# Attention and a feed-forward network on one core: the stream turned by VectorE and through DRAM ahead of the normalisation

## The chip, the cores and the metric

The kernel runs on one core of a Trainium2 chip. The metric is device time in microseconds (us), the median of several runs. A profiled execution gives a trace of every instruction on the core's engines: TensorE (PE, matrix products; PEld is its loading of weights), VectorE (DVE), ScalarE (ACT), GpSimd (POOL), and SyncE (SP), whose queue issues all the DMAs of this kernel.

## The reference, cut to what matters

The input x has 8 batches of 512 tokens and 256 features. It is normalised, and two branches work on it: a causal attention with one head (`s`), and a small transformer of two layers (`g`). The output is `x + s * silu(g)`. The 8 x 512 x 256 input runs through each layer of the transformer as follows, batch by batch:

```python
h = shift_token(x)                    # second half of the features comes from the token before
q, k, v = split(h @ wqkv)             # 8 heads of 64; q and k normalised, scaled, rotated
x = x + local_attention(q, k, v) @ wo # windows of 128 tokens, looking one window back
h = shift_token(x)
h = (h - mean) / sqrt(var + 1e-5) * lg + lb
a, g = split(h @ w1 + b1)             # 682 features each
x = x + (a * gelu(g)) @ w2 + b2
```

All arithmetic is in fp32. The change touches the step between the second `shift_token` and the product with `w1`.

## The kernel before, in words

**Layout.** The stream of one batch, `xT`, lies in SBUF with features on the 128 partitions: two chunks of 128 features, each with 512 tokens as columns. The second chunk begins one column earlier than its data, on a column of zeros, so that reading columns `c * T` to `(c + 1) * T` gives the shifted token stream at no cost. Mean and variance run over features, though, which lie on partitions; so the feed-forward must turn the stream to tokens on partitions, normalise it, and turn it back before the product with `w1`.

**The turns in the feed-forward (lines 1021 to 1191).** For each pair of token tiles (2 x 128 tokens), TensorE makes four 128x128 transposes of `xT` into a PSUM bank, `hps` (lines 1087 to 1094; the transpose itself is line 304). `layernorm` (line 438) then reads that bank: `bn_stats` and `bn_aggr` on VectorE, two small steps on GpSimd for the reciprocal root, and one `tensor_scalar` per tile on VectorE that writes `xh` in SBUF (tag `tok`, two buffers). Back it goes without TensorE, in `blocks_back` (line 1050): VectorE turns each pair in 32x32 blocks into `hn`, four DMAs write `hn` to DRAM (`hn_away`, 128 KB each), one DMA of 512 KB reads it back into `hn` with the blocks in place, and ScalarE applies gain and bias. Then come six steps of `ff` products with gelu, and two of `w2p` products, which add to the stream. The last feed-forward (batch 7, layer 1) runs in two halves and turns back on TensorE; the other fifteen work on a whole part.

**The same pattern elsewhere.** The local attention turns its q, k and probabilities this way too: VectorE in blocks, away to DRAM (`away`, `p_away`), and back in place (`qT`, `kT`, `pT`). All of these DMAs stand in SP's one queue.

**What sets the order.** The work is split into jobs written as generators; each `yield` names what its next step needs (events, free buffers, a time). The string `ORDER` (line 42) gives the order of all TensorE work: each letter is a job, and each occurrence runs it to its next `yield`; a number repeats it. A is the products with `wo` (`wop`), B the weighted sums (`ops`), C the reading back of probabilities, D the scores (`sps`), E the reading back of q and k, F the projections (`qkv`), G late loads of weights. From H on, letters are the start of a batch (normalisation and the one-head attention), the feed-forwards and the finishing steps: I is the feed-forward of batch 0, layer 0, and j that of batch 6, layer 1. I write (6,1) for batch 6, layer 1. B and D use TensorE as an array of 64x64 parts ("quarters"), the other steps use the full array.

The instructions of the other engines and the DMAs are placed by a planner, `Order.on` (line 141), at the time at which its model has their data ready; the planned order on each engine is then fixed by dependencies (`keep`, line 153). The planner's times are written in the code: `TURN_512` for a block turn of 512 columns, `LAND` for the landing of DMAs by KB (line 640), 0.42 us for an issue on SP in `send` (line 336). Each engine works through its queue in that order, so an instruction that waits holds up those behind it.

**Buffers.** There are 8 PSUM banks, one `hn`, one `hid`, two `tok`, four `xT`.

Of the kernel before, what the change touches and what calls it, by code (L numbers as in the profile page):

```python
# [15 lines left out]
P = 128  # L16
BATCH = 8
T = 512
# [21 lines left out]


ORDER = (
    "H2JH5FHFHF2JEHEF2NH3EHGHFHF3H2FH2ED2HEJ2EGF2JCFGCD2NCEF2E2J2BDCDFJEC2FEJ2EBFJDEGCJCFJFCD"
    "F2EARJEAJBGCFCJ2FEFCIJFEJ2BDGDFJGCAECEFINENCN2AI2NRNFBDIN2F2N2DN2IC3IEI5EDEBDNEI2DNF3NE"
    "F2ECDNC2ANF2ABKENCFCNCFR4DRDBERFKR2EKFEAEC2RCAKDRF2RFRKDE2F4EDEDBCFCKCECK3EBDCEDRFECFAFR"
    "FKACDEBCLCDKCFEF2BFCKCE2F3EALRD2LAKEFLCEKDBRC2FEF2LRDBELF4D2CA2ECELCL2EFLBEDODEC3F3ECLBF"
    "LA2CD2O2CF2O2CFE3FL2BCECDRFRF2EFOBDCM3EC2OMOFDEDMF2VEA2CO2EFOBC2DF2EF2BDVPOF2EV2CEAPAVFE"
    "PD2CEPOEPVFCFVOBD2FCVFEVEVEFCVECP3EBCD2VCF2A2ECFPFPEDCBDEC2F3CEFBP2FES2A2VD2E2FSPVCFC2S"
    "F2DBC2PFEVEQFVSFBDE2V2EFCQ2CQFCASVD2ESATS2F2QBEDC3DVFSZBF3S2CVEFCTFECZF2E2A2D2BT2Z2FSEZE"
    "ZC2ZCSTD2E2BZCF2ZF2CTFADCDFTZFETE2ATBEDEDF2C4FTET2FD2EWBZFCTEFECFZA2WZW3ZCFTBD2ZFE2ZCFE"  # L50
    "C2WFUFUZUEW2EUDBDZWEF2CACFCFAEZDBDZUFCFE2XCFW3CFZBDCEdDFCFXAFAWd2E2XFCdEdFBXdC2dWXD2BEX"
    "F2EdCF2dDCEDFEdA2CdFEFCX2aBC2XFDBFDdF2CFXCX2aE2dE2Fd2CaAEFdAD2EBXFD2aEC2F2CaFdEXEBC2dF2E"
    "YEaYFCFY2A2FD2BCYChF3CabFa2EaEadDBDhCFAF2EdEFCaAdb2FbDEbhDhE2aChaBDbCE2FDFCbCEbCFDBDE2C3"
    "F2hEAbFAhbFBD2CeCEF2b2FeBeF2E3C3AhAF2ehF2DEFDEFCehb2D2BFE3e2C3e2EBCD2E2eCF2A2CfFc2FhBCDE"
    "DcCFCFeFBeEhFEF2Af2AC2cEDEDFfCEheFeBCfEDChF4BfEDhFCEf2D2EcECFCfEAFAfFDiBDC3EfFEfhBEF3iAC"
    "hACiFi2FD2ChEfF2E3fDCEBDiFiCiCECi4D2BC2i2AF3gAjCjEBC2F2EFhEBjFEA2FgFjFDFEhFjDCFED2F2jCE"
    "C2EjEj2BE2CgCjFDBDCjAEjAhlDgDl2C2j2lBlglC2k2Cl4BklAkAn3lknlnm2n2mn3o2n2ono"
)


# [180 lines left out]
def gated_attention_kernel(  # L241
# [78 lines left out]
    def event(*key):  # L320
        return events.setdefault(key, {})
# [11 lines left out]
        arrived[""] = max(arrived[""], order.clock() + 2.0) + dst.free_size() * dst.shape[0] * 4 / 0.34e6  # L333
        arrived[name] = arrived[""]

    def send(dst, src, after, us):

        sync.dma_start(dst, src)
        return order.on("SP", 0.42, after) + us

    x_tiles = {}

# [92 lines left out]
    def inv_sqrt(dst, src, n):  # L435
        gpsimd.tensor_tensor(dst, src, neg_half[:, 0:n], ALU.pow)

    def layernorm(dst, src, n, name, at=0.0, groups=False):


        kind = name[0]
        few = 2 if kind == "x" else 4
        stats = small.tile([P, n, 6], F32, tag=f"stats{kind}", name=f"stats_{name}", bufs=few)
        mv = small.tile([P, n, 2], F32, tag=f"mv{kind}", name=f"mv_{name}", bufs=few)
        for i in range(n):
            vector.bn_stats(stats[:, i], src[:, i])
            end = order.on("DVE", 0.41, at, opens=f"stats{kind}")
        for i in range(n):
            vector.bn_aggr(mv[:, i], stats[:, i])
            at = order.on("DVE", 0.16, end, opens=f"mv{kind}")  # L450
        rstd = small.tile([P, n], F32, tag=f"rstd{kind}", name=f"rstd_{name}", bufs=few)
        gpsimd.tensor_scalar(rstd[:, 0:n], mv[:, 0:n, 1], EPS, None, ALU.add)
        at = order.on("POOL", 0.23, at, opens=f"rstd{kind}")
        inv_sqrt(rstd[:, 0:n], rstd[:, 0:n], n)
        at = order.on("POOL", 0.4 + 0.16 * n, at)
        for i in range(n):
            to, some = dst[:, i], src[:, i]
            if groups:
                to = to.rearrange("p (g c b) -> p c g b", g=4, c=KC)
                some = some.rearrange("p (c g b) -> p c g b", g=4, c=KC)  # L460
            vector.tensor_scalar(
                to, some, mv[:, i, 0:1], rstd[:, i : i + 1], ALU.subtract, ALU.mult
            )
            end = order.on("DVE", 0.54 if kind == "h" else 0.41, at, opens="tok" if kind == "h" else "")
        return end


# [169 lines left out]
    qTs, kTs, vs = {}, {}, {}  # L637


    TURN_512, LAND = 0.79, {64: 2.6, 128: 2.4, 256: 2.9, 384: 4.0, 512: 4.6}  # L640

    def project(b, l, t):

# [377 lines left out]
    def feed_forward(b, l, part):  # L1021
# [17 lines left out]
        def need(tag):  # L1039
            return {} if part.start else {tag: 1}  # L1040

        def behind(tag):
            return [event(tag, b, l)] if part.start else []

        def gained(dst, src, c):
            scalar.activation(
                dst, src, AF.Identity, bias=bias[:, c : c + 1], scale=gain[:, c : c + 1]
            )

        def blocks_back(hn, ends):  # L1050
# [25 lines left out]

        pairs = range(part.start // (2 * P), part.stop // (2 * P))
        yield {"after": [event("windowed", b, l, part.start), event("loaded", l, 1)]}
        yield {"after": behind("hn"), "free": need("hn") | {"tok": len(pairs)}}
        xT = stream[b]  # L1080
        hn = common("hn", [P, KC, T])
        xh = {t2: buffer("tok", [P, 2, DIM], f"xh_{b}_{l}_{t2}") for t2 in pairs}
        ends = {}
        for t2 in pairs:
            windowed = [event("windowed", b, l, t2 * 2 * P)]
            yield {"after": windowed, "free": {"bank": 1}}
            hps = bank(f"hps_{b}_{l}_{t2}").rearrange("p (a f) -> p a f", a=2)
            for a in range(2):
                t = 2 * t2 + a
                for c in range(KC):  # L1090
                    transpose(
                        hps[:, a, c * P : (c + 1) * P],
                        xT[:, c * T + t * P : c * T + (t + 1) * P],
                    )
            at = layernorm(xh[t2], hps, 2, f"h_{b}_{l}_{t2}", groups=whole_part)
            ends[t2] = at
            free(f"hps_{b}_{l}_{t2}", at)
        if whole_part:

            hn, at = yield from blocks_back(hn, ends)  # L1100
# [267 lines left out]
```

## Time and profile before

| | |
|---|---|
| time, median of 3 runs | 1326.94 us (1324.37 to 1330.78) |
| profiled execution, its own time | 1327.62 us |
| its span, first to last instruction | 1325.7 us |
| granted TensorE clock | 0.994 |
| busy: PE, DVE, ACT, POOL | 1297.2, 1041.5, 750.2, 623.8 us |
| DMA packets, bytes | 396884, 209.49 MB |

Busy times are those of one execution. A group of instructions is given with its engine and operation, what it writes and reads, its shape and count, then its busy time and the mean length of one in ns, and the idle time of the engine just before it with what ended that. Matmuls overlap in TensorE's pipeline: what one costs is read from start to start. In lists of waits the columns are the total in us, the number of times, and the longest.

### The profile page before, as it was taken

The page shows a single profiled execution, that of the slowest core. Times are in us where ns is not written, and L with a number is a line of the kernel's source. Part 1 is how long each engine was busy: PE and PEld are TensorE (multiplying, and loading weights), DVE is VectorE, ACT ScalarE, POOL GpSimd, SP SyncE. Part 2 cuts the span into 40 slices and gives each one's busy share as a digit, 9 for nine tenths or more (in the row PEclk, how much of TensorE's full clock was granted, in tenths as well). Part 3 has the DMA queues.
Part 4 walks back from the last instruction along what each step waited for, and adds up shares of the span by engine and source line. Part 5 has one row for each costly group of instructions (what it writes and reads, how often), then busy time and mean ns, then how long its engine had stood idle before and what let it go on. Part 6 is the DMA issues. An engine that isn't in the chain of part 4 may idle for free.

```text
span 1325.7 us, 29785 instructions
## 1 busy us (share of the span) xinstructions
PE 1297.2 (98%) x10498; PEld 752.9 (57%) x10498; DVE 1041.5 (79%) x3092; ACT 750.2 (57%) x1954; POOL 623.8 (47%) x651
## 2 busy tenths in 40 slices
PE   9989999999999999999999999999999999999898
PEld 4556556555555565555555655555555555555466
DVE  6778677888688987887878787788888897866764
ACT  2553554765656465563657646555655657562764
POOL 6647336564454544545543545555345354416400
PEclk9989999999999999999999999999999999999999
DMA  5878535766667564676467665575755686545662
GB/s 188 238 191 223 139 83 132 185 172 156 160 160 186 127 173 117 182 189 165 114 144 196 163 145 140 127 204 139 177 135 141 165 204 159 139 126 129 171 156 80
DMA packets 396884, 209.49 MB, mean 158 GB/s; under 512 B 153880, under 2 KB 382400, under 8 KB 396736
## 3 DMA queue, kind: packets, MB, share of 16 engines
q1 hardware_dynamic: 396736, 207.59, 62.3%
q8 instruction: 84, 1.38, 0.4%
q14 instruction: 64, 0.52, 0.1%
HBM read 111.56 MB, written 95.94 MB: 157 GB/s over the span
## 4 chain that ended last, share of the span: by engine, by line
PE 83%; DMA 6%; DVE 4%; SPq 3%; ACT 2%; POOL 2%; issue 1%; DVEq 0%; ACTq 0%
PE qkv L300 20%; PE ff L300 20%; PE w2p L300 12%; PE wop L300 7%; PE sps L300 6%; PE ops L300 5%; PE qk L300 3%; SPq L70 3%; PE av L300 2%; DMA qT<-away 2%; PE sc L300 2%; PE v0p L300 2%; DMA x<-in_x_dram 1%; PE hps L304 1%; ACT p L70 1%
## 5 line engine op out<-in xcount | busy, mean ns | idle before, releaser
L70 POOL TENSOR_TENSOR r<-r,side 128x512 f32<-128x512 f32 x128 | 162.8, 1271 | 454.4 <-DVE side L70 437.1
L300 PE MATMUL qkv<-wqkv,xT 128*128 128x512 f32 x768 | 357.8, 599 | 0.1
L300 PE MATMUL ff<-hn,w 128*128 128x512 f32 (+1 forms) x680 | 283.5, 568 | 0.0
L70 ACT ACTIVATE p<-p,nmx 128x192 f32<-128x192 f32 (+1 forms) x512 | 219.4, 429 | 89.5 <-DVE nmx L70 88.9
L300 PEld LDWEIGHTS qkv<-wqkv,xT 128*128 128x128 f32 x768 | 141.2, 191 | 140.5 <-issue 128.8
L70 POOL TENSOR_TENSOR rn<-ss,neg_half 128x8 f32<-128x8 f32 x128 | 212.9, 1664 | 10.7
L300 PEld LDWEIGHTS ff<-hn,w 128*128 128x128 f32 x680 | 128.1, 190 | 137.2 <-issue 122.8
L300 PE MATMUL w2p<-hid,w 128*128 128x512 f32 (+3 forms) x408 | 159.8, 577 | 0.0
L70 DVE CUSTOM_DVE_ANT_0 p<-sps,mask_sb 128x192 f32<-128x192 f32 (+1 forms) x512 | 146.7, 331 | 13.6 <-PE sps L300 13.3
L70 ACT ACTIVATE p<-p,rden 128x192 f32<-128x192 f32 (+1 forms) x282 | 118.6, 434 | 44.3 <-DVE rden L70 42.3
L70 DVE STREAM_TRANSPOSE pr<-p 128x384 f32<-128x384 f32 (+1 forms) x256 | 128.9, 527 | 16.7 <-ACT p L70 11.6
L70 POOL TENSOR_TENSOR r<-r,rn 128x512 f32<-128x512 f32 x128 | 134.2, 1048 | 10.0
L70 ACT ACT_TABLE_LOAD x99 | 127.0, 1283 | 4.5 <-DMA out_dram<-g 2.1
L70 ACT ACTIVATE sq<-qkv 128x512 f32<-128x512 f32 x128 | 75.2, 592 | 93.9 <-PE qkv L300 87.3
L70 DVE SCALAR_TENSOR_TENSOR hid<-ff,vec,hid 128x512 f32<-128x512 f32 (+3 forms) x119 | 83.1, 710 | 52.4 <-PE ff L300 29.9
L300 PE MATMUL wop<-oT,wo 128*128 128x256 f32 x512 | 119.1, 380 | 0.0
L300 PE MATMUL sps<-kT,qT 64*64 64x128 f32 (+1 forms) x3584 | 106.1, 255 | 11.8 <-ACT p L70 4.8
L300 PEld LDWEIGHTS sps<-kT,qT 64*64 64x64 f32 x3584 | 90.4, 136 | 44.5 <-issue 23.1
L300 PEld LDWEIGHTS w2p<-hid,w 128*128 128x128 f32 (+1 forms) x408 | 68.6, 189 | 79.5 <-issue 77.5
L300 PEld LDWEIGHTS wop<-oT,wo 128*128 128x128 f32 x512 | 96.4, 190 | 29.2 <-issue 14.7
L70 DVE TENSOR_TENSOR r<-qkv,tables 128x512 f32<-128x512 f32 x128 | 86.4, 675 | 31.5 <-ACT sq L70 29.2
L70 ACT ACTIVATE hid<-ff,vec 128x512 f32<-128x512 f32 (+2 forms) x102 | 65.7, 661 | 69.3 <-PE ff L300 68.6
(83 smaller groups left out, 1710.6 us busy)
## 6 DMA issues: line engine op xcount, KB each, us to landing
pT<-p_away SPq DMA_DIRECT2D x96, 384.0 KB, 4.3
away<-rt SPq DMA_DIRECT2D x256, 128.0 KB, 2.6
p_away<-pr SPq DMA_DIRECT2D x256, 128.0 KB, 2.3
kT<-away SPq DMA_DIRECT2D x64, 256.0 KB, 3.1
qT<-away SPq DMA_DIRECT2D x256, 64.0 KB, 2.9
p_away<-pr SPq DMA_DIRECT2D x192, 64.0 KB, 2.0
pT<-p_away SPq DMA_DIRECT2D x32, 256.0 KB, 3.3
hn_away<-hn SPq DMA_DIRECT2D x60, 128.0 KB, 2.4
```

The lines of the kernel that those rows point to most:

```text
L70: ins = getattr(self.engine, name)(*args, **kwargs)
L300: nc.tensor.matmul(out, lhsT=lhsT, rhs=rhs, start=start, stop=stop)
L304: nc.tensor.transpose(out, in_, ident)
```

## The change

For a whole part, the turn to tokens on partitions leaves TensorE. A new inner function `blocks_out` waits until both halves of the attention's output have been added to the stream. VectorE turns the two chunks of the stream in 32x32 blocks into `hn`, four DMAs write those to a DRAM tile `h_away` laid out as 512 tokens by 256 features, and two DMAs of 256 KB read it back, one per pair of token tiles, into `xh`. `layernorm` then works in place on `xh` in SBUF, for one pair after the other. The rest, `blocks_back` included, is as before. `layernorm` loses its `groups` argument, `send` gains `opens`, three landing times of the planner are changed, and `ORDER` is a new sequence over the new steps (a feed-forward on a whole part now has 15 of them, 14 before). The last feed-forward keeps its turns on TensorE.

```diff
 ORDER = (
...
-    "DcCFCFeFBeEhFEF2Af2AC2cEDEDFfCEheFeBCfEDChF4BfEDhFCEf2D2EcECFCfEAFAfFDiBDC3EfFEfhBEF3iAC"
-    "hACiFi2FD2ChEfF2E3fDCEBDiFiCiCECi4D2BC2i2AF3gAjCjEBC2F2EFhEBjFEA2FgFjFDFEhFjDCFED2F2jCE"
-    "C2EjEj2BE2CgCjFDBDCjAEjAhlDgDl2C2j2lBlglC2k2Cl4BklAkAn3lknlnm2n2mn3o2n2ono"
...
+    "f2BfA2iciEihi2F2EC2FECFhEcFfhFDBDFEF2E3fcC2i3D2CECi3giBD2C2i2FAF2AEBC3FjFEFEhBFA2j2Ejgj"
+    "F4jDF2EhDECEjDFCDh2gFCEhFEj2CBgCDCDjEjECBEjCjA2DCDl3j2lCBClglCl3klkBlA2kn3lklnkm2n4mn2o2"
+    "n2ono"
 )
...
-    def send(dst, src, after, us):
+    def send(dst, src, after, us, opens=""):
 
         sync.dma_start(dst, src)
-        return order.on("SP", 0.42, after) + us
+        return order.on("SP", 0.42, after, opens=opens) + us
...
         for i in range(n):
-            to, some = dst[:, i], src[:, i]
-            if groups:
-                to = to.rearrange("p (g c b) -> p c g b", g=4, c=KC)
-                some = some.rearrange("p (c g b) -> p c g b", g=4, c=KC)
             vector.tensor_scalar(
-                to, some, mv[:, i, 0:1], rstd[:, i : i + 1], ALU.subtract, ALU.mult
+                dst[:, i], src[:, i], mv[:, i, 0:1], rstd[:, i : i + 1], ALU.subtract, ALU.mult
             )
...
-    TURN_512, LAND = 0.79, {64: 2.6, 128: 2.4, 256: 2.9, 384: 4.0, 512: 4.6}
+    TURN_512, LAND = 0.79, {64: 2.6, 128: 2.6, 256: 3.1, 384: 4.4, 512: 4.6}
...
+        def blocks_out(hn, ends):
+
+
+            yield {"after": [event("windowed", b, l, t2 * 2 * P) for t2 in pairs]}
+            mine = hn.rearrange("p c n -> p (c n)").rearrange("p (k c a) -> p k c a", c=KC, a=32)
+            for c in range(KC):
+                src = xT[:, c * T : (c + 1) * T].rearrange("p (k a) -> p k a", a=32)
+                vector.transpose(mine[:, :, c], src)
+                at = order.on("DVE", TURN_512, opens="" if c else "hn")
+            away = dram.tile([T, DIM], F32, tag="h_away", name=f"h_away_{nm}", bufs=4)
+            rows = away.rearrange("(k a) (g n) -> g a k n", a=32, g=4)
+            mine = mine.rearrange("p k c a -> p k (c a)")
+            for g in range(4):
+                left = send(rows[g], mine[g * 32 : (g + 1) * 32], at, LAND[128])
+            tiles = away.rearrange("(t p) f -> p t f", p=P)
+            for t2 in pairs:
+                yield {"at": left - 1.0, "free": {"tok": 1}}
+                xh[t2] = buffer("tok", [P, 2, DIM], f"xh_{b}_{l}_{t2}")
+                landed = send(xh[t2], tiles[:, 2 * t2 : 2 * t2 + 2], left, LAND[256], "tok")
+                ends[t2] = layernorm(xh[t2], xh[t2], 2, f"h_{b}_{l}_{t2}", landed)
+
...
         yield {"after": [event("windowed", b, l, part.start), event("loaded", l, 1)]}
-        yield {"after": behind("hn"), "free": need("hn") | {"tok": len(pairs)}}
+        yield {"after": behind("hn"), "free": need("hn") | ({} if whole_part else {"tok": 1})}
         xT = stream[b]
         hn = common("hn", [P, KC, T])
-        xh = {t2: buffer("tok", [P, 2, DIM], f"xh_{b}_{l}_{t2}") for t2 in pairs}
-        ends = {}
-        for t2 in pairs:
...
+        xh, ends = {}, {}
+        if whole_part:
+            yield from blocks_out(hn, ends)
+        else:
+            for t2 in pairs:
...
+                at = layernorm(xh[t2], hps, 2, f"h_{b}_{l}_{t2}")
```

More of the change, by code (lines that the diff above doesn't have):

```diff
@@ L42 @@
 ORDER = (
[L43 to L54, printed above, removed]
@@ L55 @@
-    "DcCFCFeFBeEhFEF2Af2AC2cEDEDFfCEheFeBCfEDChF4BfEDhFCEf2D2EcECFCfEAFAfFDiBDC3EfFEfhBEF3iAC"
-    "hACiFi2FD2ChEfF2E3fDCEBDiFiCiCECi4D2BC2i2AF3gAjCjEBC2F2EFhEBjFEA2FgFjFDFEhFjDCFED2F2jCE"
-    "C2EjEj2BE2CgCjFDBDCjAEjAhlDgDl2C2j2lBlglC2k2Cl4BklAkAn3lknlnm2n2mn3o2n2ono"
+    "H3JH2FH3GFH2F4H2JHNEF2EHFH3EGEF3HEDHFDEHCFHJ3CDECEDFCEJFENJ2ED2BCGEJCJFJCFJFBD2CJRFJ2FCF"
+    "EGCEA2EBIJIGFJEFJC2GF2JDFBDEJCFEJFA2GI2NEN2CINRNDCN4BNDNFEIN2IEF2NCECD2NEIECI5BD2I2AF2NF"
+    "NCEFNC3FAFKFEBNCERCKR4EDBDEF3EFC2RCA2KD2FRKCF3EFEK2FBRCECFEDERBDCKFERECFCA2F2ED2RFK2EREC"
@@ new lines @@
+    "KD2BFCF2CE2KFK2BDLDRCF2ACECELCEFALFKBCDCDKRL2BECEFEF2RLC2FAFEFAFLD2EBFEF2CLFLCODCDEL2E2F"
+    "L2EBCD2ROAC2F3AEOEOFCFBEORF2D2ROE2C2FRL2BD2CFOACEMAEFCEFM3FEO2BD2CFMEF2EFVC3O2EO2DBDF3EF"
+    "EOVPAC2PVAV2P2EFV2CBDC2DOCFP2BVE2CVF2CAFED2CE2F2AFPBFE2VCP2FCSFD2FVEP2BDCDVFVC2PF2ACAPSE"
+    "BSCESECVFE2PD2BFESF2PVF2EAQC2VCV2ADS2EDFQBQ2C2TFEF3VS2CQFZSD2EBS3FEFCFEAEAET2CVTCF2D2ZVZ"
+    "FZSTZ2TZE2SBCTEDC2FDFZEZCFBDF3DEZCFETCA2E2CT2DBCDECFETF3BD2TC2FWCETFAWAE2FZCBWZCFZCTDEDB"
+    "ZFCFWTWCZEFZFAECWFAFUFZUFBD2ZFE2F2WC2UXEWCWEWUD2WFE2WZWUCdBD2ZFECZCFCEFXEAWFdADXdDXBdC2F"
@@ new lines @@
+    "WXEBCdCFE2d3CAFAFD2BdXEFECF4CdXdaEXFCEFXFDBDEFEF2X2C2AED2CdAFE2X2CFaEadDaDBEFCdCaXFCXBdF"
+    "EYF2CdYEadYCFEA2D2aCYBECYFECFEaFaFDbDdEFa2BhF2aFEFACaAEdD2EbEC3baDabDBCdCFdF2bEhEbFEBbhC"
+    "FChCFhAFEADBFDFhCECFebFEbDEDCEhb2FBECDCDEFbFCFbEA2CFEe2Fhe2BFCDCF2beDCE2BEFCEF2bD2CFE2e"
+    "A2eCeEeDBC2DcFEF2feFBD2eCeCAfAEFEFChfFEFef2CEBDC2hFeEDEBFhFhCcfFfFAD2hAECECF3fEfCfBCiDCD"
+    "f2BfA2iciEihi2F2EC2FECFhEcFfhFDBDFEF2E3fcC2i3D2CECi3giBD2C2i2FAF2AEBC3FjFEFEhBFA2j2Ejgj"
+    "F4jDF2EhDECEjDFCDh2gFCEhFEj2CBgCDCDjEjECBEjCjA2DCDl3j2lCBClglCl3klkBlA2kn3lklnkm2n4mn2o2"
@@ L436, in inv_sqrt, with layernorm @@
         gpsimd.tensor_tensor(dst, src, neg_half[:, 0:n], ALU.pow)
-    def layernorm(dst, src, n, name, at=0.0, groups=False):
+    def layernorm(dst, src, n, name, at=0.0):
         kind = name[0]
@@ L456, in layernorm @@
         for i in range(n):
-            to, some = dst[:, i], src[:, i]
-            if groups:
-                to = to.rearrange("p (g c b) -> p c g b", g=4, c=KC)
-                some = some.rearrange("p (c g b) -> p c g b", g=4, c=KC)
             vector.tensor_scalar(
-                to, some, mv[:, i, 0:1], rstd[:, i : i + 1], ALU.subtract, ALU.mult
+                dst[:, i], src[:, i], mv[:, i, 0:1], rstd[:, i : i + 1], ALU.subtract, ALU.mult
             )
-            end = order.on("DVE", 0.54 if kind == "h" else 0.41, at, opens="tok" if kind == "h" else "")
+            end = order.on("DVE", 0.54 if kind == "h" and dst is not src else 0.41, at, opens="tok" if kind == "h" and dst is not src else "")
         return end
@@ L1078, in feed_forward @@
         yield {"after": [event("windowed", b, l, part.start), event("loaded", l, 1)]}
-        yield {"after": behind("hn"), "free": need("hn") | {"tok": len(pairs)}}
+        yield {"after": behind("hn"), "free": need("hn") | ({} if whole_part else {"tok": 1})}
         xT = stream[b]
         hn = common("hn", [P, KC, T])
-        xh = {t2: buffer("tok", [P, 2, DIM], f"xh_{b}_{l}_{t2}") for t2 in pairs}
-        ends = {}
-        for t2 in pairs:
[L1085 to L1097, printed above, removed]
+        xh, ends = {}, {}
[3 more added lines that the diff above has]
+            for t2 in pairs:
+                xh[t2] = buffer("tok", [P, 2, DIM], f"xh_{b}_{l}_{t2}")
+            for t2 in pairs:
+                windowed = [event("windowed", b, l, t2 * 2 * P)]
+                yield {"after": windowed, "free": {"bank": 1}}
+                hps = bank(f"hps_{b}_{l}_{t2}").rearrange("p (a f) -> p a f", a=2)
+                for a in range(2):
+                    t = 2 * t2 + a
+                    for c in range(KC):
+                        transpose(
+                            hps[:, a, c * P : (c + 1) * P],
+                            xT[:, c * T + t * P : c * T + (t + 1) * P],
+                        )
+                at = layernorm(xh[t2], hps, 2, f"h_{b}_{l}_{t2}")
+                ends[t2] = at
+                free(f"hps_{b}_{l}_{t2}", at)
         if whole_part:
```

## The prediction

> **What bounds the kernel now.** I began with the busy shares on the profile's page:
>
> ```profile
> PE 1297.2 (98%) x10498; PEld 752.9 (57%) x10498; DVE 1041.5 (79%) x3092; ACT 750.2 (57%) x1954; POOL 623.8 (47%) x651
> ...
> q1 hardware_dynamic: 396736, 207.59, 62.3%
> ```
>
> TensorE (PE) is busy for all but 28.5 us of the 1325.7 us span. The view of busy time by stretches says where those are (columns: length, PE busy, PE loads, DVE, ACT, POOL, clock, DMA share, GB/s):
>
> ```profile
> 0.00:120.00 120.00, 108.24 (x760) 64.49 (x761) 89.05 (x270) 53.25 (x154) 77.34 (x91) 0.96 0.75 214
> 400.00:800.00 400.00, 397.67 (x3316) 229.21 (x3315) 332.08 (x985) 234.91 (x609) 192.92 (x198) 1.00 0.64 158
> 1200.00:1325.70 125.70, 116.02 (x946) 77.05 (x944) 81.47 (x223) 68.04 (x148) 37.16 (x40) 0.98 0.52 135
> ```
>
> Of the idle time 11.8 us lie in the first 120 us and 9.7 us in the last 125.7; the 1080 us between have 7.0. In the middle TensorE is the bound, and work taken from it comes back as time unless something new makes it wait. The view of waits, for TensorE alone (total, times, longest), shows which waits could grow:
>
> ```profile
> PE sps L300 <- ACT p L70: 4.8, 2, 3.6
> PE sps L300 <- DMA qT<-away: 4.6, 5, 2.0
> PE ops L300 <- DMA pT<-p_away: 4.5, 6, 1.3
> ```
>
> The wait for `hps` data (the stream, written by VectorE) is only 0.8 us in all. The groups by shape price what is removed and added, the DMA list prices the transfers (KB each, median us from issue to landing):
>
> ```profile
> L70 DVE STREAM_TRANSPOSE rt<-r 128x512 f32<-128x512 f32 x128 | 90.2, 704 | 17.4 <-POOL r L70 10.2 <-DMA away<-rt 5.9
> L70 DVE TENSOR_SCALAR xh<-hps,mv_h,rstd_h 128x256 f32<-128x256 f32 x64 | 31.5, 533 | 4.6 <-POOL rstd_h L70 4.5
> L70 DVE TENSOR_SCALAR x<-x,mv_x,rstd_x 128x256 f32<-128x256 f32 x32 | 14.4, 508 | 0.8 <-POOL rstd_x L70 0.8
> L304 PE MATMUL hps<-ident,xT 128*128 128x128 f32 x128 | 20.1, 279 | 0.8 <-DVE xT L70 0.8
> kT<-away SPq DMA_DIRECT2D x64, 256.0 KB, 3.1
> qT<-away SPq DMA_DIRECT2D x256, 64.0 KB, 2.9
> hn_away<-hn SPq DMA_DIRECT2D x60, 128.0 KB, 2.4
> ```
>
> A mean of 279 ns overstates a turn on TensorE, since they are pipelined. The timeline of TensorE gives what four of them take from start to start:
>
> ```profile
> 924.77 0.60 PE L304 MATMUL hps<-ident,xT 128*128 128x128 f32 x4
> 925.20 1.88 PE L300 MATMUL qkv<-wqkv,xT 128*128 128x512 f32 x4
> 926.92 0.60 PE L304 MATMUL hps<-ident,xT 128*128 128x128 f32 x4
> 927.45 1.57 PE L300 MATMUL sps<-kT,qT 64*64 64x128 f32 x64
> ```
>
> Four turns hold TensorE for 0.437 us (the times unrounded); before a 64x64 step 0.530.
>
> **What the Trainium skill says.** "VectorE: DVE Perf Modes", section "The three transpose paths": TensorE turns a full 128x128 into PSUM, VectorE only 32x32 blocks, into SBUF. The trace agrees: `hps` is a PSUM bank, `rt` and `hn` are SBUF tiles, and their blocks are put in place by DMA. The same page, "The perf-mode tier table", gives fp32 `tensor_scalar` from SBUF twice the rate that a PSUM source allows. The trace does not show that: 508 ns from SBUF (`x`) against 533 ns from PSUM (`xh`); I use 508. "DMA: Bandwidth & Descriptors", section "Specifications": below 512 B a transfer is under line rate. The trace agrees in direction: 64 KB in 128-byte pieces (`qT`) land in 2.9 us, 128 KB in 1 KB rows (`hn_away`) in 2.4. "Perfetto Trace Analysis", "DMA Instruction — HWDGE (DVE, Sync)": a DMA's wait is made by the sequencer that issues it. The trace agrees: SP's own queue stood 61.4 us, in 53 waits, for `away<-rt` to land.
>
> **The change, part by part.** Fifteen of the sixteen feed-forwards work on a whole part; the last keeps the old path.
>
> *Removed from TensorE:* 15 x 8 = 120 turns, 30 bursts x 0.437 = **-13.1 us**. If the dearer bursts (0.49 to 0.53) are real savings, up to -14.8; that is the low end.
>
> *The new sequence.* I went through both strings letter by letter, with the kind of TensorE work of each step. Changes between full-array and split-array work rise from 187 to 195. A visit to the 64x64 steps costs 0.12 going in or out (the first turn after `sps` starts 149 ns after the last `sps` instead of 28), 0.055 more on that burst (0.492) and 0.09 the other way (0.530 less 0.437): 0.27 for both ways, 0.13 a change. 8 x 0.13 = **+1.1 us**.
>
> *VectorE:* two more 128x512 turns per feed-forward, 30 x 0.70 = 21 us; four normalising steps per feed-forward from SBUF, 60 x (533 - 508 ns) = -1.5 us. VectorE goes from 79% to about 81%; in the stretch 400 to 800, with 332 of 400 us busy, to some 85%. I cost it at nothing on the path: its cover is the 17% that stay idle there. If that cover is gone where the masks of `sps` queue behind the two turns, each feed-forward could lose up to 1.4 us, 21 us in all (high end); nothing excludes zero.
>
> *DMA and SP:* each feed-forward had five issues (four `hn_away`, one `hn`); it gets six more, four writes and two reads, 90 in all. The trace has 1346 issues with 669 us of SP time, 0.5 us each: +45 us, SP from 50% to 54%. Packets: 2048 of 256 B and 512 of 1 KB per feed-forward, 38400. The page's 396736 packets took 62.3% of 16 engines, so 33 ns each; 38400 x 33 ns is 6 points more: 68%. Behind each SP issue stand the loads of `qT`, `kT` and `pT`, and TensorE waits for those: 9.1 us now. In the trace the landing of `qT` leads the first `sps` by a median of 3.3 us, and at a tenth of the steps by nothing, so half a microsecond of SP time is mostly absorbed. I take a quarter more on these waits, **+2 us**. Low end 0; high end one of the longest present waits, 2.0 us, in each feed-forward: +30.
>
> *Latency of the feed-forward.* In the tail (batch 6, layer 1) the trace has: last addition to the stream ends 1218.5, statistics start 1219.15, last normalising step ends 1222.8, `hn` scaled at 1233.8, in all 15.3 us. The change takes away 0.65 (turns on TensorE and the hop), and adds two turns, 2 x 0.70 and a hop, 1.5; four writes, three issues of 0.5 before the last and a landing of 2.7 (between the 2.4 of 1 KB rows and the 2.9 of 128-byte pieces), 4.3 with the hop; two reads of 256 KB, 0.5 + 3.1 = 3.6; and about 1.0 because both pairs are now normalised in a row: together +9.8, so **25 us** from the finished stream to `hn`. Is there as much other work for TensorE? I summed the steps of the new sequence between the second half's last `wop` step and the first `ff` step, each at its start-to-start time (a qkv step 1.77, `sps` 0.45 or 0.9, and so on). In the eleven feed-forwards in the middle, from (0,1) to (5,1), 33 us or more: hidden. (0,0) has 27.4, (1,0) 30.9, (7,0) 27.7, plus about 1 for changes of shape: just hidden. (6,1) has 19.7 + 0.8 = 20.5: **4.7 us of waiting**. The sequence of before has at this place a wait of 3.6 (`sps` for ACT `p`, banks not yet emptied by the softmax of four `sps` steps in close order); the new one puts other steps between those, so I take the new wait in its place: **+1.1 us**. Both together would be +4.7, neither -3.6.
>
> *Startup:* the new sequence puts the first `ops` step 3.6 us of work later, which should remove its 0.96 us wait for `pT`: **-1 us**. The buffers: `hn` is taken after the second `wop` steps, one per stage of some 80 us and held about 10 us longer; two banks fewer are claimed. I give neither a price: before, `hn` waits for nobody.
>
> Sum: -13.1 + 1.1 + 2 + 1.1 - 1 = **-9.9 us** on the profiled 1327.62 (span 1325.7 and 1.9 around it), 1317.7. That execution lies 0.7 above the median of the runs; carried over, **1317.0 us**.
>
> **Rivals.**
> *Swallowed gain (no change).* The waits grow by as much as the turns saved: the tail keeps both waits (+3.6), and (0,0), (1,0) and (7,0) miss by 2 us each, since planned latencies come late on a VectorE over 80% busy. For it: just-hidden margins of 0 to 2 us. Against: 0.7% idle in the middle now. 1317 + 3.6 + 6 = about 1326.6.
> *Slower.* SP's in-order queue: a read of the turned stream waits at its head for the writes of 256-byte pieces to land, and holds `qT` and `pT` behind it. Price: a wait as long as the longest now, 2.0 us, at one `sps` and one `ops` step of every feed-forward, less the 2 already counted: 15 x 2 x 2.0 - 2 = +58 at worst; at half of the steps +28, so 1345. It decides from 16.6 us beyond the forecast, 1.1 us per feed-forward. For it: SP stood 61 us waiting on `away<-rt`, and a tenth of the `qT` landings have no lead. Against: a median lead of 3.3 us.
> *Full gain.* No wait grows, and the tail's old one goes: 1326.9 - 14.8 - 3.6 = 1308.5. For it: the middle's waits are tiny. Against: more DMA load.
> That the turns do not leave TensorE is no rival: the code path has none.
>
> **How the numbers follow.** Forecast with its neighbours (1310 to 1320) 0.53; full gain 0.07; swallowed (1320.3 to 1333.6) 0.24; slower 0.16. A measurement tells from no change about 0.5%, 6.6 us: faster is below 1320.3. So 0.60 faster, 0.24 same, 0.16 slower. The range 1309 to 1333 leaves out the slower case and a sliver of the full gain, about 2 in 10; the forecast's own range is 1310 to 1320.
>
> **What would show it.** `hps` with 8 matmuls instead of 128; 30 more stream transposes near 0.70 us; normalising at about 508 ns; the new 128 KB writes landing in 2.4 to 2.9 us and 256 KB reads near 3.1; DMA share near 68%; PE busy near 1284 us. Between the stream's end and `hn` scaled some 25 us, and a wait of TensorE for `hn` in the last 125 us. The prediction is wrong if TensorE's waits for `qT` and `pT` rise well above 9 us in the middle, or if waits for VectorE appear there.

## The result, and the profile after

The changed kernel is slower by 0.3%: 1333.05 us, median of 20 runs (1329.08 to 1340.61), against 1329.43 us for the kernel before beside it (1324.37 to 1336.48). The ratio is 1.0031, 95% interval 1.0016 to 1.0045. A second, later set of runs gave 1.0042 (1.0028 to 1.0056). That is less than the 0.5% below which the prediction counted a time as unchanged, but on the other side from the forecast of 1317.0.

The profiled execution took 1332.94 us, with a span of 1331.0 us at a granted clock of 0.991 (before: 1325.7 us at 0.994). The page's busy shares and its DMA queue:

```profile
PE 1290.1 (97%) x10378; PEld 740.7 (56%) x10378; DVE 1052.0 (79%) x3107; ACT 744.1 (56%) x1959; POOL 625.9 (47%) x651
...
q1 hardware_dynamic: 436576, 223.32, 66.8%
```

120 matmuls have gone from TensorE, as the change says. Span less busy time was 28.5 us before; it is 40.9 us now. TensorE's busy time fell by 7.1 us (1297.2 to 1290.1), its idle time rose by 12.4, and the span grew by the difference, 5.3. The stretches (length, PE busy, PE loads, DVE, ACT, POOL, clock, DMA share, GB/s) show where:

```profile
0.00:120.00 120.00, 109.36 (x785) 65.04 (x786) 95.81 (x291) 56.90 (x171) 80.54 (x95) 1.00 0.79 219
400.00:800.00 400.00, 395.56 (x3266) 224.36 (x3265) 325.67 (x948) 229.68 (x592) 190.91 (x196) 1.00 0.68 170
120.00:1200.00 1080.00, 1062.06 (x8648) 597.66 (x8647) 871.27 (x2588) 622.41 (x1641) 507.46 (x517) 0.99 0.68 167
1200.00:1331.00 131.00, 118.69 (x947) 77.96 (x945) 84.91 (x229) 64.79 (x147) 37.92 (x40) 0.96 0.52 137
```

The startup has 10.6 us without a busy TensorE (11.8 before) and the tail 12.3 (9.7). The 1080 us between went from 7.1 to 17.9. So most of the new idle time lies in the long middle that was called full. Of the waits of TensorE (total, times, longest) these are the largest:

```profile
PE sps L301 <- DMA qT<-away: 10.0, 7, 4.6
PE sps L301 <- ACT p L71: 5.9, 1, 5.9
PE ops L301 <- DMA pT<-p_away: 5.5, 7, 1.5
```

No wait for `hn` is among them. TensorE waits for the attention's loads, 9.1 us for `qT` in the middle alone, where it was 0.5. Now the groups of instructions that are new or changed, with idle time ahead of them at the end:

```profile
L71 DVE STREAM_TRANSPOSE hn<-xT 128x512 f32<-128x512 f32 x30 | 19.5, 682 | 0.0
L71 DVE TENSOR_SCALAR xh<-xh,mv_h,rstd_h 128x256 f32<-128x256 f32 x60 | 30.2, 543 | 4.3 <-POOL rstd_h L71 3.8
L71 DVE BATCH_NORM_STATS2 stats_h<-xh 128x6 f32<-128x256 f32 x60 | 22.3, 413 | 17.5 <-DMA xh<-h_away 17.4
```

The last line is the one to keep in mind: VectorE stood 17.4 us with the statistics at the head of its queue, waiting for the turned stream to land. The list of DMAs (KB each, median us from issue to landing) has the trip and the loads that share the queue with it:

```profile
qT<-away SPq DMA_DIRECT2D x256, 64.0 KB, 3.0
kT<-away SPq DMA_DIRECT2D x64, 256.0 KB, 3.3
h_away<-hn SPq DMA_DIRECT2D x60, 128.0 KB, 3.1
xh<-h_away SPq DMA_DIRECT2D x30, 256.0 KB, 3.8
```

And SP stands for the turned blocks as well. Its wait on VectorE's `hn`, before and after, each from the list of SP's waits:

```profile
SPq L70 <- DVE hn L70: 10.8, 6, 3.4
```

```profile
SPq L71 <- DVE hn L71: 55.2, 16, 9.5
```

### The profile page after: what moved, and what is told of

Its sections match the earlier page's. It is cut to its first block, busy times and chain, and to the rows that moved or that the text cites. A ratio compares the mean times of both kernels' runs of the same rounds, so it can differ in the third digit from the quotient of the medians.

```text
span 1331.0 us, 29689 instructions
## 1 busy us (share of the span) xinstructions
PE 1290.1 (97%) x10378; PEld 740.7 (56%) x10378; DVE 1052.0 (79%) x3107; ACT 744.1 (56%) x1959; POOL 625.9 (47%) x651
## 3 DMA queue, kind: packets, MB, share of 16 engines
q1 hardware_dynamic: 436576, 223.32, 66.8%
## 4 chain that ended last, share of the span: by engine, by line
PE 76%; DMA 8%; DVE 6%; SPq 4%; POOL 2%; ACT 2%; issue 1%; DVEq 0%; ACTq 0%; POOLq 0%
PE ff L301 22%; PE qkv L301 18%; PE w2p L301 9%; PE wop L301 7%; PE sps L301 5%; PE ops L301 5%; SPq L71 4%; PE qk L301 3%; DMA xh<-h_away 2%; PE sc L301 2%; DMA qT<-away 2%; PE av L301 2%; DMA x<-in_x_dram 1%; DMA away<-rt 1%; PE v0p L301 1%
## 5 line engine op out<-in xcount | busy, mean ns | idle before, releaser
L71 DVE STREAM_TRANSPOSE rt<-r 128x512 f32<-128x512 f32 x128 | 90.2, 705 | 29.8 <-POOL r L71 18.8
```

The costliest lines, as they stand in the source:

```text
L71: ins = getattr(self.engine, name)(*args, **kwargs)
```

## The experiments

Three theories stood at the start. **S**: the six DMAs of the trip cost what the turns save. **O**: another chain is the bound, and TensorE's turns were free. **N**: the new sequence is worse by itself. A fourth, **M**, was formed after the first four runs: the sequence only fits one set of planned times, and an edit that shifts them costs time of its own. In every run that takes away the turns, the trip or a wait for either, the turn to tokens on partitions is left out of what is normalised: the normalisation reads the stream as it lies, or as it was sent, in tiles of the same size. Ratios are to the kernel before on the same chip, with the 95% interval.

**The first four: one part at a time, planner left to plan.** The kernel before without turns on TensorE:

```diff
-                    transpose(
-                        hps[:, a, c * P : (c + 1) * P],
-                        xT[:, c * T + t * P : c * T + (t + 1) * P],
-                    )
-            at = layernorm(xh[t2], hps, 2, f"h_{b}_{l}_{t2}", groups=whole_part)
+                ends[t2] = layernorm(xh[t2], Unturned(xT, t2), 2, f"h_{b}_{l}_{t2}", order.clock(), groups=True)
```

> The kernel before with its own sequence; the four turns per pair on TensorE are left out for the fifteen whole-part feed-forwards, and the normalisation reads the unturned stream in SBUF instead, so what it normalises is not the reference's. Nothing is added. Theory S (the six new DMAs stand in SP's queue ahead of the loads of q, k and probabilities, and take back what TensorE saved): 13 us less than before, about 0.990 of it. Theory O (another chain binds as soon as TensorE has less to do, whatever is added): within 4 us of before, 0.997 to 1.0. Theory N (the new sequence by itself leaves less lead): like S, 0.990.

Measured 0.9995 (0.9982 to 1.0008). The changed kernel without its DMAs, normalising the turned blocks where they lie:

```diff
-            for g in range(4):
-                left = send(rows[g], mine[g * 32 : (g + 1) * 32], at, LAND[128])
...
-                landed = send(xh[t2], tiles[:, 2 * t2 : 2 * t2 + 2], left, LAND[256], "tok")
-                ends[t2] = layernorm(xh[t2], xh[t2], 2, f"h_{b}_{l}_{t2}", landed)
+                src = hn[:, :, t2 * 2 * P : (t2 + 1) * 2 * P]
+                ends[t2] = layernorm(xh[t2], src, 2, f"h_{b}_{l}_{t2}", at)
```

> The changed kernel with its new sequence and its two block turns on VectorE, but without the way through DRAM: the normalisation reads the turned blocks where they lie, so the blocks are not in place. Theory S: 1315 to 1320 on before's 1329, ratio about 0.990. Theory O: as the changed kernel, 1.000 to 1.003. Theory N: as the changed kernel, 1.000 to 1.003; VectorE's two turns as the cause would show the same.

Measured 1.0112 (1.0081 to 1.0144): leaving six DMAs out made the kernel slower. The new sequence with the old turns on TensorE in place of `blocks_out`'s body:

```diff
-                vector.transpose(mine[:, :, c], src)
...
+                    for c in range(KC):
+                        transpose(
+                            hps[:, a, c * P : (c + 1) * P],
+                            xT[:, c * T + t * P : c * T + (t + 1) * P],
+                        )
+                ends[t2] = layernorm(xh[t2], hps, 2, f"h_{b}_{l}_{t2}", groups=True)
```

> The new sequence with the old turns on TensorE (each pair turned in the step where the changed kernel reads it back); no new DMA, no new turn on VectorE; it computes the reference. Theory S: the sequence is sound, so about before, 0.998 to 1.003. Theory N: the changed kernel's waits come back on top of the old work, about 1.010 to 1.013. Theory O: 0.998 to 1.003.

Measured 1.0084 (1.0060 to 1.0109). And the kernel before with the six DMAs added:

```diff
+                for g in range(4):
+                    mine = xT[g * 32 : (g + 1) * 32, 0 : 2 * T].rearrange("p (k n) -> p k n", n=64)
+                    left = send(rows[g], mine, order.clock() + 1.6, LAND[128])
+                for i in pairs:
+                    send(unused, tiles[:, 2 * i : 2 * i + 2], left, LAND[256])
```

> The kernel before with its own sequence and turns, plus six DMAs per whole-part feed-forward of the changed kernel's sizes on SP (four writes of 128 KB in 256-byte pieces, two copies of 256 KB, here from DRAM to DRAM), on which nothing waits. Theory S: 8 to 18 us more than before, 1.006 to 1.013. Theories O and N: at most 3 us more, 1.000 to 1.002.

Measured 1.0200 (1.0171 to 1.0229), above what any theory had. These four do not answer the question. Each edit changes what the planner knows, it then orders VectorE, ScalarE, GpSimd and SP anew for the whole kernel, and the string `ORDER`, made for other times, stays. So from here on every kernel keeps the planned order of each engine: a removed instruction still takes its place in the plan without being issued, an added one is put into the queue without pushing others in the plan.

**Orders kept: the turns, and the trip.** The kernel before, its turns planned and not made:

```diff
                 for c in range(KC):
+                    if whole_part:
+                        order.took(0.11, turns=True)
+                        continue
                     transpose(
...
-            at = layernorm(xh[t2], hps, 2, f"h_{b}_{l}_{t2}", groups=whole_part)
+            src = Unturned(xT, t2) if whole_part else hps
+            at = layernorm(xh[t2], src, 2, f"h_{b}_{l}_{t2}", groups=whole_part)
```

> The kernel before, with the order on every engine exactly as it was: the planner still counts the turns, but TensorE doesn't make them, and the normalisation reads the unturned stream, so its values are not the reference's. Theory M (a sequence fits one set of planned times; the first experiments shifted the planned orders, and that cost what they lost): the 13 us now appear, ratio 0.989 to 0.993. Theory O (another chain binds): 0.998 to 1.001.

Measured 0.9929 (0.9909 to 0.9949). The same edit gave 0.9995 with the planner left to plan. O falls: time taken from TensorE comes back, 9.4 us here. For this edit M holds. The changed kernel with the six DMAs planned and not issued, VectorE's two turns still made:

```diff
-                left = send(rows[g], mine[g * 32 : (g + 1) * 32], at, LAND[128])
+                left = order.on("SP", 0.42, at, ghost=True) + LAND[128]
...
-                landed = send(xh[t2], tiles[:, 2 * t2 : 2 * t2 + 2], left, LAND[256], "tok")
-                ends[t2] = layernorm(xh[t2], xh[t2], 2, f"h_{b}_{l}_{t2}", landed)
+                landed = order.on("SP", 0.42, left, opens="tok", ghost=True) + LAND[256]
+                ends[t2] = layernorm(xh[t2], Unturned(xT, t2), 2, f"h_{b}_{l}_{t2}", landed, True)
```

> The changed kernel with every order kept, but the six DMAs per feed-forward are not issued; VectorE still makes its two turns, and the normalisation reads the unturned stream at the place where the changed kernel has it, so values are not the reference's. Theory S (the six DMAs cost what the turns save): 0.990 to 0.994 of before. Theory O: 0.999 to 1.003, as the changed kernel.

Measured 0.9906 (0.9884 to 0.9927), 1317.95 us. The middle of that kernel is full again:

```profile
120.00:1200.00 1080.00, 1071.12 (x8786) 604.15 (x8789) 877.20 (x2603) 625.62 (x1646) 518.54 (x528) 1.00 0.63 155
```

8.9 us idle against 17.9. N falls: the new sequence costs no time that shows. It has waits of its own, though, as TensorE's list for these 1080 us says:

```profile
PE sps L311 <- DMA qT<-away: 7.0, 4, 3.6
```

So of the 9.1 us for `qT` in the middle of the changed kernel (0.5 before), most come with the sequence and not with the trip. The trip, with everything that waits for it, is worth 15 us by the medians (1333.05 less 1317.95); but these were measured beside different runs of the kernel before (1329.43 and 1330.65), and by the ratios, 1.0031 less 0.9906, it is some 17 us. VectorE's turns cost nothing that shows by their length. Then the other way round, the six DMAs put into SP's queue of the kernel before, with nobody waiting for them:

```diff
+                    sync.dma_start(rows[g], mine)
+                    left = order.on("SP", 0.0, order.clock() + 1.6 + 0.42 * g) + 0.42 + LAND[128]
...
+                    sync.dma_start(unused, tiles[:, 2 * i : 2 * i + 2])
+                    order.on("SP", 0.0, left + 0.42 * i)
```

> The kernel before with every other instruction in its place, and the six DMAs of each feed-forward put into SP's queue at the times at which the changed kernel's planner would have them (the two reads as copies from DRAM to DRAM); nothing waits for them. Theory S: 8 to 20 us more, 1.006 to 1.015. Theory M (most of the 27 us of the first such experiment came from shifted orders): at most 1.003.

Measured 1.0148 (1.0121 to 1.0175). TensorE's waits in that kernel:

```profile
PE sps L300 <- DMA qT<-away: 17.9, 9, 7.9
PE ops L300 <- DMA pT<-p_away: 7.1, 11, 1.9
```

`qT` was at 4.6 and `pT` at 4.5 in the kernel before. DMAs that nobody waits for are paid for by the loads behind them. M, which allowed 1.003 at most, fails here: most of what the first such addition cost (1.0200) is the DMAs' own. No engine that computes waits for these six, but SP does: it stands until the stream that they send is written (7.6 us before), and until the writes have landed that the reads need (none before):

```profile
SPq L70 <- DVE xT L70: 16.6, 7, 5.3
SPq L70 <- DMA h_away<-xT: 9.4, 8, 2.3
```

**Issues, packets, bytes.** The same six DMAs with 32 pieces of 256 bytes each (8 KB), so that the issues remain and the traffic goes:

```diff
-                    sync.dma_start(rows[g], mine)
+                    sync.dma_start(rows[g][:, 0:1], mine[:, 0:1])
...
-                    sync.dma_start(unused, tiles[:, 2 * i : 2 * i + 2])
+                    sync.dma_start(unused[0:32, 0, 0:64], tiles[0:32, 0, i * 64 : (i + 1) * 64])
```

> As the one with the trip's six DMAs added and all orders kept, but each moves only 32 pieces of 256 bytes, so SP issues as often and next to nothing is moved. If SP's issue time is what costs: as with the full DMAs. If it is the traffic on the DMA engines: at most 1.003.

Measured 1.0054 (1.0033 to 1.0075). In the kernel before, 90 more issues are thus worth some 7 us and the traffic some 12 (0.0094 of 1329). Then the full bytes, but the writes in pieces of 1 KB, 512 packets per feed-forward instead of 2048:

```diff
-                    sync.dma_start(rows[g], mine)
+                    sync.dma_start(away[g * 128 : (g + 1) * 128].rearrange("(a k) n -> a k n", a=32), xT[g * 32 : (g + 1) * 32, 0 : 2 * T].rearrange("p (k n) -> p k n", n=DIM))
```

> As the run that adds the six full DMAs to the kernel before with orders kept, but the four writes go out in 1 KB pieces in place of 256 bytes: same bytes, same issues, 512 packets instead of 2048. If the number of packets makes the traffic's share of the cost: close to the small DMAs' 1.005, at most 1.009. If the bytes do: about 1.015 again.

Measured 1.0076 (1.0051 to 1.0100). Most of the traffic's price goes with the number of packets, not the bytes. How it acts is not separated: SP's wait for the writes to land is shorter too (5.2 us with 1 KB pieces, 1.5 with 8 KB, against 9.4), while the median landing of `qT` is 3.0 us and that of `kT` 3.1 in all three kernels. In the changed kernel itself, the writes as one 4 KB piece per partition (the blocks then are not put in place):

```diff
-            rows = away.rearrange("(k a) (g n) -> g a k n", a=32, g=4)
-            mine = mine.rearrange("p k c a -> p k (c a)")
+            rows = away.rearrange("(g a k) f -> g a (k f)", g=4, a=32)
+            mine = mine.rearrange("p k c a -> p (k c a)")
```

> The changed kernel, every order, issue and byte kept, but the four writes of the turned stream go out as one 4 KB piece per partition instead of sixteen of 256 bytes; the blocks are then not put in place, so its values are not the reference's. If the 256-byte pieces are the larger part of the trip's 15 us (the run with 1 KB pieces gave 10 us back): 1322 to 1327 us, 0.994 to 0.998 of before. If the bytes or the wait for the way through DRAM cost: 1.001 to 1.004, as the changed kernel.

Measured 0.9994 (0.9978 to 1.0011), a little less gained than the first range said: some 5 us of the 15 to 17 came back, so packets alone are not the answer for the changed kernel.

**Another queue.** If SP's queue is the trouble, another one might carry the trip. ScalarE's first:

```diff
+    def send_by_act(dst, src, after, us, opens=""):
+
+        left = order.on("SP", 0.42, after, opens=opens, ghost=True)
+        scalar.dma_start(dst, src)
+        order.besides("ACT", left - 0.42)
+        return left + us
...
-                left = send(rows[g], mine[g * 32 : (g + 1) * 32], at, LAND[128])
+                left = send_by_act(rows[g], mine[g * 32 : (g + 1) * 32], at, LAND[128])
...
-                landed = send(xh[t2],
+                landed = send_by_act(xh[t2],
```

> The changed kernel with every planned order kept, but the six new DMAs of each feed-forward issued by ScalarE's queue in place of SP's, at the planned times. If SP's issue time is a part of the cost (7 us by the run with small DMAs), that part comes back: 0.996 to 0.999 of before, 1325 to 1329 us. If only the traffic costs: 1.001 to 1.004, as the changed kernel. If ScalarE, which now waits in line for those DMAs, becomes the hold-up: above 1.005.

Measured 1.0192 (1.0172 to 1.0212). TensorE's waits there:

```profile
PE sps L311 <- DMA qT<-away: 18.8, 7, 5.9
PE av L311 <- ACT pT L71: 7.2, 5, 3.1
```

`av` waits 7.2 us for ScalarE, 2.6 in the changed kernel: the issues stand in ScalarE's queue until the blocks are turned or have landed, and hold the activations behind them. The largest such wait in ScalarE's list:

```profile
ACT p L71 <- DMA h_away<-hn: 9.9, 3, 5.9
```

The five DMAs of the way back, in the kernel before, moved in the same manner:

```diff
-                there = send(rows[s], mine, at, LAND[128])
+                there = send_by_act(rows[s], mine, at, LAND[128])
...
-            landed = send(hn.
+            landed = send_by_act(hn.
```

> The kernel before, orders kept, but the five DMAs of each feed-forward that it has already (four that write the turned hn, one that reads it back) issued by ScalarE's queue. If SP's queue holds TensorE up already in the kernel before: 3 to 8 us less, 0.994 to 0.998. If SP only binds above its present load: 0.999 to 1.002.

Measured 1.0133 (1.0116 to 1.0151), a miss of the same kind. Last GpSimd, with the trip as above but `gpsimd.dma_start`:

```diff
-                left = send(rows[g], mine[g * 32 : (g + 1) * 32], at, LAND[128])
+                left = send_by_pool(rows[g], mine[g * 32 : (g + 1) * 32], at, LAND[128])
...
-                landed = send(xh[t2],
+                landed = send_by_pool(xh[t2],
```

> The changed kernel, its six DMAs per feed-forward issued by GpSimd (47% busy) in place of SP, all planned orders kept. If the issues on SP cost what the additions to before say, some 7 us come back: 0.996 to 0.999. If an in-order engine that computes is held up by such issues as ScalarE was (1.0192), above 1.005.

Measured 1.0305 (1.0283 to 1.0327), the dearest. GpSimd's waits on the trip:

```profile
POOL h_away L71 <- DVE hn L71: 32.2, 5, 18.3
POOL xh L71 <- DMA h_away<-hn: 23.2, 8, 5.7
```

Its busy time also rose from 625.9 to 690.0 us, and a write landed after 4.0 us instead of 3.1. The page lists the DMAs of GpSimd's queue as another kind (`software_dynamic`, 5280 packets), so this run changes more than the queue. An engine with half its time idle is not a free queue: it stands in order too.

**Dividing the trip's price in the changed kernel.** The trip stays in SP's queue with all its bytes, but its writes take the stream itself, its reads go to an unused tile, and the normalisation reads the unturned stream. Nobody waits for the trip, and it does not wait for the turns:

```diff
-                left = send(rows[g], mine[g * 32 : (g + 1) * 32], at, LAND[128])
+                flat = xT[g * 32 : (g + 1) * 32, 0 : 2 * T].rearrange("p (k n) -> p k n", n=64)
+                left = send(rows[g], flat, at, LAND[128])
...
-                landed = send(xh[t2], tiles[:, 2 * t2 : 2 * t2 + 2], left, LAND[256], "tok")
-                ends[t2] = layernorm(xh[t2], xh[t2], 2, f"h_{b}_{l}_{t2}", landed)
+                landed = send(unused, tiles[:, 2 * t2 : 2 * t2 + 2], left, LAND[256], "tok")
+                ends[t2] = layernorm(xh[t2], Unturned(xT, t2), 2, f"h_{b}_{l}_{t2}", landed, True)
```

> The changed kernel with every planned order kept; the six DMAs of each feed-forward are still issued by SP with all their bytes and 256-byte pieces, but the writes take the stream itself and the reads go to an unused DRAM tile, and the normalisation reads the unturned stream: nobody waits for the trip, and the trip does not wait for VectorE's turns (so the normalisation is of unturned data). If the waits for the trip (SP standing 55.2 us for VectorE's hn, the normalisation for its landing) carry the cost, the ratio to before falls to 0.991 to 0.996; if issues and traffic carry it, it stays at 1.000 to 1.005.

Measured 0.9975 (0.9963 to 0.9987). The same with 8 KB per DMA:

```diff
-                left = send(rows[g], flat, at, LAND[128])
+                left = send(rows[g][:, 0:1], flat[:, 0:1], at, LAND[128])
...
-                landed = send(unused, tiles[:, 2 * t2 : 2 * t2 + 2], left, LAND[256], "tok")
+                landed = send(unused[0:32, 0, 0:64], tiles[0:32, 0, t2 * 64 : (t2 + 1) * 64], left, LAND[256], "tok")
```

> As the idle trip in the changed kernel, but each of the six DMAs moves only 32 pieces of 256 bytes (8 KB). What lies between this run and the one without the trip (0.9906) is the price of 90 issues on SP, what lies between this run and the idle trip is the price of packets and bytes. From the additions to the kernel before (7 and 11 us) I expect 0.995 to 0.997.

Measured 0.9922 (0.9904 to 0.9941), and the changed kernel on that chip:

> The changed kernel itself, on the chip of these runs, for their differences: 1.002 to 1.005.

Measured 1.0042 (1.0028 to 1.0056). Neither theory of the idle trip had it right alone: waits carry 0.0067, packets and bytes 0.0053, with what SP stands for them in its own queue (7.0 us for the writes to land in the idle trip, 3.0 with 8 KB). Two more kernels take one of the waits away each. Writes from the stream, so that SP does not stand for the turns, with the normalisation still waiting for the reads:

```diff
-                left = send(rows[g], mine[g * 32 : (g + 1) * 32], at, LAND[128])
+                flat = xT[g * 32 : (g + 1) * 32, 0 : 2 * T].rearrange("p (k n) -> p k n", n=64)
+                left = send(rows[g], flat, at, LAND[128])
```

> The changed kernel with one wait less: the four writes send the stream itself, so SP does not wait for VectorE's two turns (which are still made); the normalisation still waits for the two reads (and works on unturned data). If SP standing for the turns (55.2 us, with the loads of qT, kT and pT behind it) makes the 9 us between the changed kernel (1.0042) and the idle trip (0.9975), this falls to 0.997 to 0.999; if the normalisation's wait for its landing does, it stays at 1.003 to 1.005.

Measured 1.0012 (0.9999 to 1.0025). The writes from the turned blocks, with nobody waiting for the reads:

```diff
-                landed = send(xh[t2], tiles[:, 2 * t2 : 2 * t2 + 2], left, LAND[256], "tok")
-                ends[t2] = layernorm(xh[t2], xh[t2], 2, f"h_{b}_{l}_{t2}", landed)
+                landed = send(unused, tiles[:, 2 * t2 : 2 * t2 + 2], left, LAND[256], "tok")
+                ends[t2] = layernorm(xh[t2], Unturned(xT, t2), 2, f"h_{b}_{l}_{t2}", landed, True)
```

> The opposite half: the four writes send the turned blocks and SP waits for VectorE's turns as in the changed kernel, but the reads go to an unused DRAM tile and the normalisation reads the unturned stream at once. If SP standing for the turns carries the 9 us: 1.003 to 1.005; if the late normalisation does: 0.997 to 0.999.

Measured 0.9989 (0.9975 to 1.0003). Again between the two theories: both waits seem to count, the normalisation's probably more; what SP's wait gives back is hardly clear of the intervals. What each of the two kernels still waits for shows that the edits hit what they aimed at. First the one that does not wait for the turns, VectorE's wait for the landing from its list:

```profile
DVE stats_h L71 <- DMA xh<-h_away: 17.5, 13, 3.2
```

It is as long as in the changed kernel, while SP's wait for `hn` (the writes of the way back are left in it) has fallen from 55.2 us:

```profile
SPq L71 <- DVE hn L71: 34.1, 11, 9.2
```

Then the one in which nobody waits for the reads; the wait for the landing is gone from VectorE's groups:

```profile
L80 DVE BATCH_NORM_STATS2 stats_h<-xT 128x6 f32<-128x256 f32 x60 | 22.0, 407 | 0.0
```

Taking 1.0036, the middle of the changed kernel's two results, and 1329 us for the kernel before:

| what is taken from the changed kernel | ratio | worth, us |
|---|---|---|
| SP's wait for the turns | 1.0012 | 3 |
| the normalisation's wait for its landing | 0.9989 | 6 |
| both | 0.9975 | 8 |
| and the packets and bytes | 0.9922 | 7 more |
| and the issues (no trip at all) | 0.9906 | 2 more |

The last three rows add up to 17 us. Each worth is uncertain by 2 to 4 us, from the intervals, and the last cannot be told from nothing. That the issues are cheaper here than in the kernel before (7 us) is within what these intervals allow.

## Why the prediction was wrong

**What was right.** The turns are worth what the prediction took, 13.1 us of TensorE's time. The page of the kernel before without its turns, orders kept, has 1297.2 less 13.1:

```profile
PE 1284.1 (97%) x10378; PEld 741.0 (56%) x10378; DVE 1041.0 (79%) x3092; ACT 749.6 (57%) x1954; POOL 625.1 (47%) x651
```

The changed kernel itself misses the 1284 us that were named as a sign: it has 1290.1, at a clock of 0.991. Without the trip it is 1288.5, at the same clock as in the line above (0.992), so the sequence costs TensorE some 4 us of busy time where 1.1 were taken, by one execution of each; the time of the kernel does not show it. The kernel without the trip ended at 1317.95, ratio 0.9906; the forecast without its 2 us for DMA is 1315.0 on 1326.94, ratio 0.991. Startup gave 1.2 us where 1 was foretold, in part by luck: it is what is left of several waits, of which that for `qT` fell most (4.2 to 0.8 us), and not `pT`'s alone. A block turn took 682 ns (0.70), DMA's share is 66.8% (68), packets rose by 39840 (38400). From the finished stream of batch 6, layer 1, to the scaled `hn` it took 27.1 us where 25 was worked out; the writes land after 3.1 us instead of 2.7, the reads after 3.8 instead of 3.1, and the normalising step took 543 ns, not 508, so that it is no faster from SBUF than it was from PSUM.

**The step that failed: "DMA and SP", +2 us, with "VectorE" at nothing beside it.** They were worth some 17 us together. The prediction priced the added issues as a quarter more of the waits that the trace named, 9.1 us, because `qT` lands with a median lead of 3.3 us. SP's issue time did grow as foretold, by 61 us (669 to 730) where 45 were worked out, and the issues alone, at 8 KB each, cost the changed kernel some 2 us, what the prediction took for the whole term. The error is what comes with them. Three parts of the price were missing or too small:

- *The wait at the head of VectorE's queue* (some 6 us). The prediction covered VectorE's new work by its idle time, and asked of the landing only whether TensorE has other work meanwhile. It has, and TensorE never waits for `hn`. But the statistics stand in VectorE's queue until the reads land, 17.4 us in 14 waits, and what is queued behind them is the attention's turns (`rt`, `pr`), whose DMAs feed `qT` and `pT`. Idle time on an engine covers new work, not a new wait at the head of its queue. The chain of work that ended last in the changed kernel shows this path in places: it passes through the landing of `xh` seven times, 27.6 us or 2.1% of the span (four times, 15.7 us, in the second trace of the same kernel), and goes on through the statistics and what stands behind them, as in the tail below. How much of the 6 us went this way is not shown. The run without that wait shows its price by its median only: in its trace, of an execution 3.4 us above that median, TensorE's waits for `qT` and `pT` are no shorter (15.9 and 7.6 us).
- *SP's wait for VectorE's turns* (some 3 us, hardly clear of noise). 10.8 us before, 55.2 after. But 32.5 us are there without the trip, for the writes of the way back in the new sequence, so some 21 to 23 us are the trip's. The rival "slower" had a wait at the head of SP's queue, but of the reads for the writes to land; that one is only 7.0 us, in 5 waits. The wait that counts is one step ahead of it.
- *The 256-byte packets* (some 7 us, with the bytes and SP's wait for their landing). Counted correctly, and then given no price beyond the share of 68%.

**The tail.** A wait of 4.7 us for `hn` was foretold in place of one of 3.6. There is one of 5.9 us, but TensorE does not stand for `hn`. SP's queue after the change, with the load at its end (start, length):

```profile
1220.30 2.44 SPq L71 DMA_DIRECT2D h_away<-hn  x4
1222.85 2.32 SPq L71 DMA_DIRECT2D away<-rt  x4
1225.93 0.96 SPq L71 DMA_DIRECT2D xh<-h_away  x2
1227.86 2.32 SPq L71 DMA_DIRECT2D qT<-away  x4
```

and TensorE's step that needs it:

```profile
1232.26 2.08 PE L301 MATMUL sps<-kT,qT 64*64 64x128 f32 x32 [5.91 <-ACT p L71]
```

The wait is put down to ScalarE's `p`, and two things that the trip delays end there almost together. One is the load: by the trace's semaphores the four `qT` landed between 1231.9 and 1232.5. Before the change that load was issued 1.5 us earlier, at 1226.35, with nothing of the trip ahead of it. The other is `p` itself, which ended at 1232.15. The chain that ended last leads back from it (start, length):

```profile
1225.93 3.66 DMA xh<-h_away
1229.59 0.02 issue
1229.61 0.75 DVE stats_h L71 x2
...
1231.43 0.17 DVE p L71
1231.61 0.02 DVE nmx L71
1231.63 0.02 issue
1231.65 0.50 ACT p L71 x2
1232.15 0.10 issue
1232.26 2.08 PE sps L301 x27
```

VectorE's mask of the scores (`p`, `nmx`), which ScalarE needs, stands behind the statistics, and these wait for the turned stream to land. Which of the two ended the 5.9 us the trace does not tell; the trip stands ahead of both. The wait for `hn` that was foretold never comes up.

**The rivals.** "Swallowed gain" gave about 1326.6, by late feed-forwards; the measured time is 6 us above that, just past the end of the prediction's range (1333.05 against 1333.0), and the feed-forwards were not late for TensorE. "Slower" had the right kind of mechanism, an in-order queue that holds `qT` and `pT`, and nearly twice its price: +28 beyond the forecast, where +16 came. (2.5 of the 16 are the starting point: the kernel before had 1329.43 beside the changed one, where the forecast set out from 1326.94.) The sign that the prediction itself named against it, waits for `qT` and `pT` well above 9 us in the middle, was met: 12.6 us there (1.8 before), 15.5 in all. It shows the trip only in part, since 7.2 of the 12.6 are there in the kernel without the trip too.

**What stays open.** Whether a sequence made anew for a lighter trip would beat the kernel before was not tried; none of the kernels run here that does the whole computation was faster than it.

## What to carry to other kernels

Price an added DMA by what stands behind its issue in its queue, and the instruction that waits for it by what stands behind that in its engine's queue; idle time covers neither. The cheapest test of such a price is to add the DMAs with nobody waiting for them. It tells the sign better than the size: it gave 20 us in the kernel before (1.0148) and 9 in the sequence made for the trip (0.9975 less 0.9906). Where a fixed sequence is paired with a planner that orders the other engines, keep every planned order in an experiment: the same edit gave 0.9995 with the plan redone and 0.9929 with it kept.

## What the runs showed of the hardware beyond that

The length of pieces shows in the landing as well as in the price: a 128 KB write of the trip landed after 2.4 us in 4 KB pieces, 2.5 in 1 KB pieces and 2.9 to 3.3 in 256-byte pieces. Moving six DMAs per feed-forward from SP, which computes nothing, to an engine that computes cost more than it gave on both engines tried, 1.0192 on ScalarE and 1.0305 on GpSimd, though these are busy for 56% and 47% of the span. The granted clock of the profiled executions went roughly with the time: 0.991 to 0.995 at spans up to 1327.5 us, 0.989 to 0.994 from there to 1334.5, 0.985 to 0.991 at 1336 to 1357, 0.981 at the longest, 1372.8. PE's busy time tends to rise as it falls, for the same matmuls: the two traces of the changed kernel have 1290.1 us at 0.991 and 1296.2 at 0.988, with 10378 matmuls each. That part of a difference is named by no wait. Whether the waits lower the clock was not tested.
